# Six of fifteen sums of exps made by accumulating DMAs, in a fused graph network and masked attention kernel

## The chip, the cores and the metric

The kernel runs on one core of a Trainium2 chip. The metric is the device time of one execution in microseconds (us); the time of a kernel is the median of its runs. The engines are TensorE (PE: matmuls; PEld: its weight loads), VectorE (DVE), ScalarE (ACT), GpSimd (POOL) and SyncE (SP, here the issuer of most DMAs). They run side by side, each executing its own instructions in order, and wait for one another through semaphores.

## What is computed

Two layers over x of shape 8 x 2048 x 256 in float32. Layer 0 is a graph convolution with two linear maps and batch norms, layer 1 attention over the graph's edges with 4 heads of 64; each has a residual and a layer norm. The change is in layer 1:

```python
qkv = h @ W                                  # q, k, v: 8 x 4 heads x 2048 x 64
mask = jnp.where(adj == 0, -jnp.inf, 0.0)
scores = jnp.einsum('bhid,bhjd->bhij', q, k) / np.sqrt(HEAD_DIM) + mask
attn = jax.nn.softmax(scores, axis=-1)
out = jnp.einsum('bhij,bhjd->bhid', attn, v)
x = _layernorm(x + out, axis=-1)
```

The softmax needs, for each query, the sum of the exps over all 2048 keys. That sum is what the change moves about.

## The kernel before

The first 1270 us or so are layer 0, which the change doesn't touch. The attention then runs over NU = 64 units (8 batches x 2 pairs of heads x 4 chunks of 512 queries). A unit goes through NT = 16 tiles of 128 keys. Scores are made transposed, keys on the partitions and queries along the free dimension, for two heads at a time, so that a tile of exps, `prob`, is 128 x 2 x 512 float32: 4 KB in each partition, 512 KB in all. The sum over the keys is thus a sum over 16 tiles and then over 128 partitions.

For each step g (tile j of unit u) these functions are issued, in an order written out by hand in the main loop, and every engine keeps it:

- `scores(g + 3)` (L824): four matmuls of 64 x 64 tiles, keys times queries, into PSUM (`st`, two buffers). Scores run LEAD = 3 tiles ahead.
- `mask_scores(g + 3)` (L836): VectorE adds the mask while it takes the scores out of PSUM into a `prob` buffer; there are 13 of these.
- `exps(g + 3)` (L842): ScalarE, in place.
- side tasks, listed by unit and step in `side`: projections of later q, k and v (L765, L779), layer norms, loads, and the end of the unit before.
- `weigh(g)` (L854): TensorE multiplies the exps by v and accumulates in PSUM (`out_ps`). In the last step of a unit it comes before the masks of that step.
- `add_up(g)` (L863, L865): GpSimd adds tile after tile into `acc` (two buffers).

The end of a unit is `finish_sums(u)` at step 4 of the next unit. There TensorE multiplies by a matrix of ones, which sums over the partitions. It does so for every part of the sum that is left: `acc`, and those tiles that GpSimd did not add, whose number is `on_pe(u)`. Each part is four matmuls with 32 columns of ones and 256 columns of data (L881); a float32 matmul shows as two instructions in the records, so a part is 8 of them. ScalarE then copies the sums out (L889), and two steps on they are turned, inverted and applied to the output (L895 to L916). At step 4 after the last unit the same is done for unit 63, with nothing beside it.

So `on_pe` divides the 16 tiles: the first `16 - on_pe(u)` go to GpSimd, the rest to TensorE. Before, it is 4 for the last three units and 1 for all others: a usual unit has 14 adds on GpSimd (tiles 0 to 14) and two parts on TensorE (tile 15 and `acc`).

A `prob` buffer is used again for the tile 13 further on: the mask of tile g + 3, issued in step g, writes into the buffer of tile g - 10, and waits for all that read or write that.

Of the kernel before, what the change touches and what calls it, by code (L numbers as in the profile page):

```python
# [11 lines left out]
ALU = mybir.AluOpType  # L12
# [14 lines left out]
def tile_gcn_then_masked_attention(  # L27
# [15 lines left out]
    nc = tc.nc  # L43
# [7 lines left out]
    NT = N // P  # L51
# [4 lines left out]
    NCH = N // CH  # L56
# [138 lines left out]
    with tc.tile_pool(name="bt7", bufs=1, side="right") as bp7, tc.tile_pool(  # L195
# [20 lines left out]
        for n, t in enumerate(order):  # L216
# [7 lines left out]
            j, m = divmod(t, HT)  # L224
            k, q = divmod(m, TPC)
            here = slice(q * P, (q + 1) * P)
            for g in range(NT // 4):
# [4 lines left out]
                i, m0 = divmod(4 * g, HT)  # L232
# [405 lines left out]
    NU = B * HP * NCH  # L638
# [156 lines left out]
    def attention():  # L795


        with tc.tile_pool(
# [9 lines left out]
            units = [(b, hp, c) for b in range(B) for hp in range(HP) for c in range(NCH)]  # L808
            probs, accs, outs, ots, sts, pms = {}, {}, {}, {}, {}, {}

            def on_pe(u):

                return 4 if u >= NU - NCH + 1 else 1

            def scores(g):
                u, j = divmod(g, NT)
# [40 lines left out]
                        )  # L857

            def add_up(g):
                u, j = divmod(g, NT)  # L860
                if j == 1:
                    accs[u] = ap_.tile([P, 2, CH], F32, name="acc")
                    nc.gpsimd.tensor_add(accs[u], probs[g - 1], probs[g])  # L863
                elif 1 < j < NT - on_pe(u):
                    nc.gpsimd.tensor_add(accs[u], accs[u], probs[g])  # L865

            def finish_out(u):
                ots[u] = ap_.tile([P, CH], F32, name="ot")
                nc.scalar.copy(ots[u], outs[u][:, 0, :])
                nc.vector.tensor_add(ots[u], outs.pop(u)[:, 1, :], ots[u])  # L870

            def finish_sums(u):

                pm = ps_m.tile([P, BR], F32, name="pm")
                parts = [probs.pop(g) for g in range((u + 1) * NT - on_pe(u), (u + 1) * NT)]
                parts.append(accs.pop(u))
                for n, part in enumerate(parts):
                    for h in range(2):
                        for q in range(2):
                            r0 = 32 * (2 * h + q)  # L880
                            nc.tensor.matmul(  # L881
                                pm[r0 : r0 + 32, :], ones[:, :32],
                                part[:, h, q * BR : (q + 1) * BR],
                                start=(n == 0), stop=(n == len(parts) - 1),
                            )
                for g in range(u * NT, (u + 1) * NT - on_pe(u)):
                    del probs[g]
                sts[u] = ap_.tile([P, BR], F32, name="sm")
                nc.scalar.copy(sts[u], pm)  # L889
# [64 lines left out]
            for b in range(B):  # L954
# [3 lines left out]
                for c in range(NCH):  # L958
# [3 lines left out]
                    u = u0 + 3 + c  # L962
# [26 lines left out]
            with tc.manual_schedule(engines=IN_ORDER):  # L989
# [34 lines left out]
                for g in range(NU * NT):  # L1024
                    u, j = divmod(g, NT)
                    ahead = g + LEAD < NU * NT
                    if ahead:
                        st = scores(g + LEAD)
                    if j == NT - 1:
                        weigh(g)  # L1030
                        finish_out(u)
                    if ahead:
                        mask_scores(g + LEAD, st)
                        exps(g + LEAD)
                    for _, f, args in side.get((u, j), ()):
                        f(*args)
                    if j < NT - 1:
                        weigh(g)
                    add_up(g)
# [5 lines left out]
    def attention_with_maxima():  # L1045

        with tc.tile_pool(name="full", bufs=2) as ap_, tc.tile_pool(
# [9 lines left out]
            for b in range(B):  # L1057
# [55 lines left out]
                for c in range(NCH):  # L1113
# [3 lines left out]
                    for half in range(2):  # L1117
                        inp.emit(b, c, half)

    attention()  # L1120


# [62 lines left out]
```

## Time and profile before

| | before |
|---|---|
| median of three runs | 3640.62 us (3638.4 to 3642.35) |
| span of the profiled execution | 3639.4 us |
| TensorE busy | 3587.3 us, 99% |
| GpSimd busy | 2757.1 us, 76% |
| VectorE busy | 1989.5 us, 55% |
| ScalarE busy | 1642.6 us, 45% |
| GpSimd adds into acc (L863, L865) | 887, of 2.36 us each |
| matmul records of L881 on prob / on acc | 584 / 512 |

Busy shares are over the whole span; engines do different things in its parts, so the table of stretches, which gives busy times between two points in time, is the one to argue from. In a line of a group the columns are: source line, engine, operation, output and inputs by the program's names, shapes, number of instructions, and after the bar the busy time in us, the mean of one in ns, and the idle time of the engine just before them with what ended most of it. Timelines give start and length in us; consecutive instructions of one kind are merged. The ends of matmuls are modelled and overlap with what follows, so that differences of starts are the better measure on TensorE.

### The profile page before, as it was taken

What the parts mean: (1) busy time and instruction counts of PE and PEld (TensorE: products, weight loads), DVE (VectorE), ACT (ScalarE), POOL (GpSimd) and SP (SyncE); (2) the same over time, 40 slices, a digit from 0 to 9 for tenths busy, and PEclk for the clock granted to TensorE, in tenths of its full rate; (3) what the DMA queues carried; (4) which work ended last, traced back from release to release, by engine and by line L of the source; (5) the groups of instructions that cost most, each with busy time, mean ns of one, the idle gap of its engine ahead of it and who ended that gap; (6) DMA issues with size and microseconds to landing.
All of it is one profiled execution on the core that took longest, in us unless ns stands there. A gap on an engine that the chain in (4) does not pass through costs nothing.

```text
span 3639.4 us, 55807 instructions
## 1 busy us (share of the span) xinstructions
PE 3587.3 (99%) x23055; PEld 1487.6 (41%) x23055; DVE 1989.5 (55%) x2929; ACT 1642.6 (45%) x2036; POOL 2757.1 (76%) x1457
## 2 busy tenths in 40 slices
PE   8999999999999899999999999999999999999997
PEld 4444444444444443433343433343433334343332
DVE  6212141221146646766766766676676676676665
ACT  5001100110135455655665665565566566556554
POOL 3443263424247678999999999999999999999996
PEclk9999999999999899999999999999999999999998
DMA  9122232230256300000010010010001000000000
GB/s 338 61 75 87 81 133 81 75 98 29 81 204 252 147 1 7 24 30 13 19 42 13 13 36 24 13 36 24 7 30 36 7 24 30 13 19 24 7 1 25
DMA packets 132761, 205.82 MB, mean 57 GB/s; under 512 B 6912, under 2 KB 113936, under 8 KB 122000
## 3 DMA queue, kind: packets, MB, share of 16 engines
q1 hardware_dynamic: 132032, 196.11, 15.6%
q0 software_dynamic: 288, 4.98, 0.4%
q8 instruction: 183, 3.00, 0.3%
q10 hardware_dynamic: 176, 1.06, 0.1%
q14 instruction: 82, 0.67, 0.1%
HBM read 126.62 MB, written 75.51 MB: 56 GB/s over the span
## 4 chain that ended last, share of the span: by engine, by line
PE 96%; POOL 1%; DVE 1%; ACT 1%; DMA 0%; issue 0%; SPq 0%; POOLq 0%; DVEq 0%; ACTq 0%
PE out_ps L854 25%; PE st L824 24%; PE pa L329 21%; PE pm L765 6%; PE ph L362 5%; PE pa L539 5%; PE pm L779 3%; PE pm L881 2%; PE pm L707 1%; PE pm L733 1%; PE ps L231 1%; PE pm L908 1%; PE pm L895 1%; POOL acc L865 1%; PE ph L584 1%; PE pc L241 0%
## 5 line engine op out<-in xcount | busy, mean ns | idle before, releaser
L865 POOL TENSOR_TENSOR acc<-acc,prob 128x1024 f32<-128x1024 f32 x823 | 1947.5, 2366 | 97.8 <-ACT prob L842 40.6
L836 DVE SCALAR_TENSOR_TENSOR prob<-mask,st 128x1024 f32<-128x1024 uint8 x1024 | 1243.3, 1219 | 616.9 <-PE st L824 582.0
L842 ACT ACTIVATE prob<-prob 128x1024 f32<-128x1024 f32 x1024 | 1082.3, 1057 | 945.4 <-DVE prob L836 925.1
L854 PE MATMUL out_ps<-prob,v 64*64 64x512 f32 x8192 | 1077.1, 596 | 1.7 <-DVE ot L870 1.7
L824 PE MATMUL st<-qt,kt 64*64 64x512 f32 x8192 | 1064.2, 590 | 0.1
L329 PE MATMUL pa<-t,x 128*128 128x512 f32 x1792 | 773.2, 594 | 2.7 <-ACT x L305 2.7
L824 PEld LDWEIGHTS st<-qt,kt 64*64 64x64 f32 x8192 | 312.8, 133 | 566.9 <-issue 528.3
L329 PEld LDWEIGHTS pa<-t,x 128*128 128x128 f32 x1792 | 341.3, 191 | 432.6 <-issue 428.4
L854 PEld LDWEIGHTS out_ps<-prob,v 64*64 64x64 f32 x8192 | 284.9, 132 | 511.6 <-issue 412.7
L410 POOL TENSOR_TENSOR ag<-ag,dbc 128x512 f32<-128x512 f32 x16 | 20.2, 1262 | 486.1 <-DVE ag L409 456.6
L366 ACT ACTIVATE h<-ph,b1s 128x512 f32<-128x512 f32 x112 | 77.0, 688 | 404.4 <-PE ph L362 404.4
L765 PE MATMUL pm<-x1t,wq 128*128 128x512 f32 x512 | 247.2, 606 | 0.7 <-ACT x1t L739 0.7
L390 ACT COPY ag<-pa 128x512 f32<-128x512 f32 x16 | 9.4, 586 | 422.7 <-PE pa L329 411.6
L362 PE MATMUL ph<-ag,w1s 128*128 128x512 f32 x448 | 193.4, 592 | 0.0
L863 POOL TENSOR_TENSOR acc<-prob 128x1024 f32<-128x1024 f32 x64 | 151.2, 2362 | 32.5 <-ACT prob L842 31.0
L668 ACT ACTIVATE x<-x,ln_nm,ln_rs 128x256 f32<-128x256 f32 x256 | 137.4, 586 | 9.3 <-POOL ln_nm L664 9.3
L779 PEld LDWEIGHTS pm<-wq,x1t 128*128 128x128 f32 x1024 | 119.3, 192 | 29.3 <-issue 27.3
L367 DVE BATCH_NORM_STATS2 st<-h 128x6 f32<-128x512 f32 x112 | 76.9, 692 | 99.1 <-ACT h L366 99.1
L362 PEld LDWEIGHTS ph<-ag,w1s 128*128 128x128 f32 x448 | 85.1, 190 | 107.1 <-issue 106.9
L779 PE MATMUL pm<-wq,x1t 128*128 128x128 f32 x1024 | 128.4, 278 | 0.3 <-ACT x1t L739 0.3
L765 PEld LDWEIGHTS pm<-x1t,wq 128*128 128x128 f32 x512 | 88.2, 192 | 95.9 <-issue 89.1
L299 POOL TENSOR_TENSOR x<-x,dinv 128x1024 f32<-128x1024 f32 x60 | 116.7, 1966 | 0.0
(137 smaller groups left out, 2425.3 us busy)
## 6 DMA issues: line engine op xcount, KB each, us to landing
x<-in_x_dram SPq DMA_DIRECT2D x92, 512.0 KB, 4.1
h_d<-h SPq DMA_DIRECT2D x28, 1024.0 KB, 3.9
t<-h_d SPq DMA_DIRECT2D x28, 1024.0 KB, 7.9
a<-in_adj_dram SPq DMA_DIRECT2D x16, 1024.0 KB, 5.1
y_d<-ag SPq DMA_DIRECT2D x32, 512.0 KB, 2.7
out_dram<-x SPq DMA_DIRECT2D x32, 512.0 KB, 2.9
yt<-y_d SPq DMA_DIRECT2D x28, 512.0 KB, 3.2
bt_d<-t SPq DMA_DIRECT2D x4, 2048.0 KB, 16.1
```

Of the source, the lines that this page charges most:

```text
L329: nc.tensor.matmul(pa, s.t[:, m, :], t[:, m, :], start=(m == 0), stop=(m == HT - 1))
L362: nc.tensor.matmul(ph, w1s[:, d, f * P : (f + 1) * P], ag[:, d, :], start=(d == 0), stop=(d == ND - 1),)
L539: nc.tensor.matmul(py, w[:, f, :], t[:, f, :], start=(f == 0), stop=(f == 1))
L668: nc.scalar.activation(self.t[:, i, :], self.t[:, i, :], AF.Identity, bias=self.nm[:, i : i + 1], scale=self.rs[:, i : i + 1],)
L765: nc.tensor.matmul(pm, wq[:, d, wcols], xt[:, d, cols], start=(d == 0), stop=(d == ND - 1))
L779: nc.tensor.matmul(pm[:, j * P : (j + 1) * P], xt[:, d, t * P : (t + 1) * P], wq[:, d, wcols], start=(d == 0), stop=(d == ND - 1),)
L824: nc.tensor.matmul(st[r * HD : (r + 1) * HD, h, :], kt[hs, j * P + r * HD : j * P + (r + 1) * HD], qt[hs, cols], start=True, stop=True,)
L836: nc.vector.scalar_tensor_tensor(p, mask[:, j, cols][:, None, :].to_broadcast([P, 2, CH]), MASKED, st, op0=ALU.mult, op1=ALU.add,)
L842: nc.scalar.activation(probs[g], probs[g], AF.Exp)
L854: nc.tensor.matmul(outs[u][hs, r, :], inp.qkv[b, hp][2][rs, j, hs], probs[g][rs, h, :], start=(j == 0), stop=(j == NT - 1),)
L863: nc.gpsimd.tensor_add(accs[u], probs[g - 1], probs[g])
L865: nc.gpsimd.tensor_add(accs[u], accs[u], probs[g])
```

## The change

TensorE gets the `acc` part alone in every unit but the last: `on_pe` becomes 0, and 4 for unit 63. All sixteen tiles are then in GpSimd's sum. To make room on GpSimd, six pairs of tiles, (2, 3), (4, 5) up to (12, 13), are first added to each other by the DMA engines: GpSimd issues a DMA from the second tile's buffer to the first's, SBUF to SBUF, with `accum_op=ALU.add`, and adds the pair's sum to `acc` three steps later. Tiles 0 and 1 start `acc` as before, and tiles 14 and 15 are added one by one. The pair (12, 13) is added in step 0 of the next unit. In unit 63 it is five pairs, up to (10, 11), and tiles 12 to 15 go to TensorE.

The DMA for the pair i, i + 1 overwrites tile i. It stands on GpSimd's queue at step i + 1 and waits for TensorE to have weighed tile i and for ScalarE's exp of tile i + 1. The add of the pair waits for the DMA to have landed.

```diff
+            PAIRS = range(2, NT - 2, 2)
+
             def on_pe(u):
-
-                return 4 if u >= NU - NCH + 1 else 1
+                return 4 if u == NU - 1 else 0
...
             def add_up(g):
+
                 u, j = divmod(g, NT)
+                here = NT - on_pe(u)
                 if j == 1:
                     accs[u] = ap_.tile([P, 2, CH], F32, name="acc")
                     nc.gpsimd.tensor_add(accs[u], probs[g - 1], probs[g])
-                elif 1 < j < NT - on_pe(u):
+                elif j - 1 in PAIRS and j < here:
+                    nc.gpsimd.dma_start(probs[g - 1], probs[g], accum_op=ALU.add)
+                elif PAIRS[-1] + 1 < j < here:
                     nc.gpsimd.tensor_add(accs[u], accs[u], probs[g])
+
+                v, i = divmod(g - 4, NT)
+                if v >= 0 and i in PAIRS and i + 1 < NT - on_pe(v):
+                    nc.gpsimd.tensor_add(accs[v], accs[v], probs[g - 4])
```

## The prediction

> **What bounds the kernel now.** I read the page's busy shares first, then a table of stretches, then the chain of waits, then the timelines of TensorE and GpSimd inside one unit.
>
> Busy shares, on the page:
>
> ```profile
> PE 3587.3 (99%) x23055; PEld 1487.6 (41%) x23055; DVE 1989.5 (55%) x2929; ACT 1642.6 (45%) x2036; POOL 2757.1 (76%) x1457
> ```
>
> The attention stretch alone, from the table of stretches (us, then busy time of PE, PEld, DVE, ACT, POOL, each with its count of instructions):
>
> ```profile
> 1350.00:3560.00 2210.00, 2208.78 (x18777) 871.06 (x18779) 1500.62 (x2213) 1305.31 (x1549) 2093.95 (x1074) 1.00 0.06 20
> ```
>
> TensorE is without gaps there (2208.78 of 2210) and GpSimd comes next (2093.95, 95%). VectorE has 68%, ScalarE 59%, the DMA engines 6%. The chain that ended last is 96% PE and 1% POOL. So time is gained only by taking work from TensorE, and GpSimd has no room for it as it stands.
>
> The costliest groups on GpSimd:
>
> ```profile
> L865 POOL TENSOR_TENSOR acc<-acc,prob 128x1024 f32<-128x1024 f32 x823 | 1947.5, 2366 | 97.8 <-ACT prob L842 40.6
> L863 POOL TENSOR_TENSOR acc<-prob 128x1024 f32<-128x1024 f32 x64 | 151.2, 2362 | 32.5 <-ACT prob L842 31.0
> ```
>
> 14 adds of 2.366 us are 33.1 us of a unit. The TensorE timeline where a unit's sums are taken, first in a usual unit, then in unit 62 (start, length):
>
> ```profile
> 1999.86 1.04 PE L824 MATMUL st<-qt,kt 64*64 64x512 f32 x8
> 2000.83 0.64 PE L881 MATMUL pm<-prob,ones 128*32 128x256 f32 x8
> 2001.29 0.61 PE L881 MATMUL pm<-acc,ones 128*32 128x256 f32 x8
> 2001.83 1.09 PE L854 MATMUL out_ps<-prob,v 64*64 64x512 f32 x8
> ```
> ```profile
> 3594.15 1.93 PE L881 MATMUL pm<-prob,ones 128*32 128x256 f32 x32
> 3595.90 0.61 PE L881 MATMUL pm<-acc,ones 128*32 128x256 f32 x8
> 3596.45 1.09 PE L854 MATMUL out_ps<-prob,v 64*64 64x512 f32 x8
> ```
>
> Starts tell what a part costs: two parts hold TensorE from 2000.83 to 2001.83, 1.00 us; five from 3594.15 to 3596.45, 2.30 us. One part more or less is (2.30 - 1.00) / 3 = 0.433 us. A usual unit, from one such place to the next, takes 35.5 to 37.5 us; the last units, with no projection beside them, about 30.7 with two parts (from 3531.52 to 3562.19).
>
> What the trace shows of DMAs: two issued by GpSimd (its timeline), and landing times (us, last column of the list of issues).
>
> ```profile
> 1240.33 0.96 POOL L628 DMA_DIRECT2D wq<-in_L_gnn_W_dram  x1
> 1241.30 0.58 POOL L629 DMA_DIRECT2D mask<-mask_d  x1
> ```
> ```profile
> y_d<-ag SPq DMA_DIRECT2D x32, 512.0 KB, 2.7
> wq<-in_L_gnn_W_dram POOLq DMA_DIRECT2D x1, 768.0 KB, 4.8
> ```
>
> No DMA before goes SBUF to SBUF, and none adds.
>
> **What the Trainium skill says.** (1) "DMA: Bandwidth & Descriptors", SWDGE vs HWDGE vs iDMA: accumulating is only to be had from GpSimd's queue, where its own cores write the descriptors. The trace agrees that an issue costs GpSimd time: 0.96 and 0.58 us. (2) Same page, Anatomy of one DMA: about 2.0 us fixed plus bytes at 436 GB/s, which gives 3.2 us for 512 KB as a plain copy; the trace has 2.7 us for a copy of that size issued by SyncE, and 4.8 us against a formula's 3.8 for GpSimd's 768 KB. (3) "Collectives: The Full Stack", The bandwidth ceiling: an add in the DMA path costs no cycles of its own but needs two source reads on one ring, so half the rate. Nothing before shows it. (4) "SBUF — State Buffer", Who interferes with whom: DMAs have ports of their own and don't slow engines. Not shown here for such traffic.
>
> **The change part by part.**
>
> *Parts of the sums on TensorE.* Before, units 0 to 60 gave TensorE one tile beside acc, units 61 to 63 four. After, only unit 63 gives four. Removed: 61 x 1 + 2 x 4 = 69 parts of 0.433 us = 29.9 us, all on the path, since TensorE has no gaps. Does a stall take its place? The next out_ps matmuls need exps that were started three tiles earlier (5.2 us at 1.72 us a tile, against a chain of 1.22 us on VectorE and 1.06 on ScalarE), so no.
>
> *GpSimd's adds.* 887 before. After, a full unit has 1 + 6 + 2 = 9 adds, 9 x 2.366 = 21.3 us, and six issues. I take 0.8 us an issue (both ends 0.58 and 0.96 seen for 128 rows or so; up to 1.5 if the second read needs more descriptors), 4.8 us. With the LayerNorm root of 1.8 us that some units have, it is 27.9 us against a unit of 35.1. Busy time is not the limit; order and waits are.
>
> *The new waits.* The DMA for pair i stands at step i+1 and waits for TensorE to have read tile i (it overwrites it) and for the exp of tile i+1. The add of pair i stands three steps later and waits for the landing. GpSimd runs in order, so behind a late landing stand the next DMA issue and the next adds; behind those VectorE (13 prob buffers) and TensorE, which wants acc at step 4 of the next unit.
>
> *Landing time L, from start of issue.* Bytes: 512 KB over 16 engines is 32.8 KB each. The page's main queue moved 196.11 MB in 15.6% of 16 x 3639 us, 21.6 GB/s an engine, so a pass is 1.5 us at most; I take 1.4. Fixed share: 2.7 - 1.4 = 1.3 us for SyncE's copy, to which GpSimd's 0.8 us of descriptors is added, 2.1; or 4.8 - 2.1 = 2.7 from the wq load. One pass gives L = 3.5 to 4.1, two passes (the skill's two reads) 4.9 to 5.5, three passes in series 6.3 to 6.9. I take two passes, L = 5.0.
>
> *GpSimd's sequence over a unit with L = 5.0*, from the issue for pair 2, at the last units' pace of 3.44 us a pair: issues start at 0, 3.44, 7.37, 10.8, 14.7 and 19.0 at the latest; the first add waits until 5.0 and ends at 7.4, the next start at landings 8.4, 12.4, 15.8; then pair 12's issue and five adds in a row (tiles 14, pair 10, 15, pair 12, and the next unit's first), to 30.8, 32.6 with the LayerNorm root. Each us on L adds some 2.25 us to this chain, since two DMAs are in flight and half of the wait shows at each of the pairs.
>
> A usual unit takes TensorE 35.5 - 0.43 = 35.1 us: the chain of 32.6 hides, 2.5 us to spare. The last three or four units take 30.7 - 0.43 = 30.2: there GpSimd falls back by 2.4 us a unit. Some 3.5 units make 8 us that TensorE waits for acc, the last of it just before the final sums (now acc's last add starts at 3611.9 and TensorE's sums at 3614.8, near already).
>
> *VectorE and ScalarE.* Same instructions; a mask's write into a prob buffer waits for a landing instead of a GpSimd add, six steps after the pair's add is due, some 10 us. Cost nothing.
>
> *Sum:* 3640.6 - 29.9 + 8 = 3619 us.
>
> **The rivals.**
>
> *A, slower: the landings become GpSimd's bound.* If the add reads and writes in series, or its rate is lower, L = 6.6 (three passes): the chain is 32.6 + 2.25 x 1.6 = 36.2, 1.1 us over each of 60 usual units = 66, and 6 us over 3.5 last ones = 21; 3640.6 - 29.9 + 87 = 3698. With L = 7.5 it is 3.1 x 60 + 28 - 29.9, about 3825. For it: nothing before shows such a DMA, and the sequence leaves just 1.1 us of L. Against it: the DMA engines are 6% busy there, and the page on reduction says that the add itself is free.
>
> *B, no change.* L near 6.1 (chain 35.1, last units 17 us late), or an issue of 2 us: the 29.9 us are eaten, 3635 to 3645.
>
> *C, all hidden.* One pass, L at most 4: the chain is 30.3, as short as the last units; 3640.6 - 29.9 = 3611.
>
> **How the numbers follow.** The forecast with two passes 0.56, C 0.17, B 0.06, A 0.21. The likeliest is 3619. Low end: C less 2 us of run-to-run spread (3638.4 to 3642.35 before), 3609. High end: into A up to L of about 6.5, 3690; left out are C's lower edge and A beyond it, near 2 in 10. Faster by over 0.2% (below 3633.3) is the forecast and C, 0.73; within, B, 0.06; slower, A, 0.21.
>
> **What would show it right or wrong.** L881 with prob falls from 584 matmul records to some 32, and TensorE's sums take 0.57 us a unit. GpSimd shows 573 adds of 2.37 us, and 383 issues of about 0.8 us that land in about 5 us. Usual units take about 35.1 us. In the last three, adds that wait for landings and a TensorE gap of 2 to 4 us before L881's acc. Wrong: landings above 6 us, GpSimd idle before pair adds in every unit with TensorE waiting for acc; an issue of over 1.5 us; adds or masks that grow longer beside the DMAs.

## The result, and the profile after

| | before | after |
|---|---|---|
| median | 3641.3 us (3638.4 to 3642.35) | 3625.68 us (3622.14 to 3625.93) |
| ratio after / before | | 0.9956, 95% interval 0.9939 to 0.9973 |
| span of the profiled execution | 3639.4 us | 3623.8 us |

The change makes the kernel faster by 15.6 us, 0.44%. A second measurement of the same two kernels gave 3638.62 and 3623.64 us, ratio 0.9954 (0.9940 to 0.9968).

Busy shares of the changed kernel, and its attention stretch in the table of stretches (busy time of PE, PEld, DVE, ACT, POOL):

```profile
PE 3561.4 (98%) x22503; PEld 1470.9 (41%) x22503; DVE 1990.5 (55%) x2929; ACT 1638.1 (45%) x2036; POOL 2357.3 (65%) x1526
```
```profile
1350.00:3560.00 2210.00, 2206.02 (x18498) 863.22 (x18494) 1518.46 (x2243) 1315.29 (x1565) 1728.96 (x1150) 1.00 0.53 108
```

TensorE still has no gaps to speak of in the long middle (2206 of 2210 us), so it still bounds, with less to do. GpSimd fell from 2094 to 1729 us there. The DMA engines went from 6% to 53% busy, and VectorE's and ScalarE's instructions are as long as before (page: a mask 1219 ns, an exp 1057 ns in both kernels). The groups of instructions on GpSimd, and the DMAs with their time to landing:

```profile
L877 POOL TENSOR_TENSOR acc<-acc,prob 128x1024 f32<-128x1024 f32 x383 | 944.9, 2467 | 133.6 <-DMA prob<-prob 123.2
L871 POOL DMA_DIRECT2D prob<-prob x383 | 337.7, 883 | 359.0 <-PE out_ps L858 262.9
L873 POOL TENSOR_TENSOR acc<-acc,prob 128x1024 f32<-128x1024 f32 x126 | 317.2, 2518 | 4.9
```
```profile
prob<-prob POOLq DMA_DIRECT2D x383, 512.0 KB, 4.6
```

An issue holds GpSimd for 0.883 us and lands 4.6 us after it began; that is the median, and single landings in the trace take up to 7.4 us. The adds' means of 2.47 and 2.52 us are no slowing: in the timeline below, an add that follows an issue is recorded as starting before the issue's end (2.66 us from 2003.48, where the issue runs to 2003.75), and those that follow a wait take 2.36 or 2.37. One stretch of GpSimd's timeline in a usual unit:

```profile
2002.88 0.87 POOL L871 DMA_DIRECT2D prob<-prob  x1 [2.17 <-PE out_ps L858]
2003.48 2.66 POOL L877 TENSOR_TENSOR acc<-acc,prob 128x1024 f32<-128x1024 f32 x1
2006.31 0.87 POOL L871 DMA_DIRECT2D prob<-prob  x1 [0.17 <-issue]
2007.94 2.37 POOL L877 TENSOR_TENSOR acc<-acc,prob 128x1024 f32<-128x1024 f32 x1 [0.76 <-DMA prob<-prob]
```

Both waits of the new scheme are to be seen: GpSimd waits for TensorE before it may overwrite a tile, and for landings before it adds. In a usual unit neither reaches TensorE.

**Where the time went.** TensorE's timeline, from the start of one unit's sums to the next, unit beside unit in both kernels:

| stretch | after less before, us |
|---|---|
| up to unit 0's sums | -0.4 |
| 60 units: 60 x -0.43 | -25.8 |
| 8 of these 60 units longer than that | +3.1 |
| units 61 to 63 up to the final sums: parts | -3.9 |
| the same: TensorE stalls, and slower matmuls after one of them | +6.9 |
| final sums, up to the transposes behind them | +2.1 |
| from there to the last instruction | +0.2 |
| last instruction to the end of the span | +2.2 |
| sum | -15.6 |

The saving of 29.7 us (25.8 + 3.9) is there; 14 us of it are given back, most of them at the kernel's end. TensorE there (second number: length; in brackets: idle before, and what ended it):

```profile
3543.84 0.44 PE L907 MATMUL pm<-ident,sm 128*128 128x128 f32 x2 [0.91 <-ACT sm L901]
...
3570.53 0.64 PE L893 MATMUL pm<-acc,ones 128*32 128x256 f32 x8 [0.55 <-POOL acc L877]
...
3578.20 0.44 PE L907 MATMUL pm<-ident,sm 128*128 128x128 f32 x2 [3.44 <-ACT sm L901]
...
3579.01 1.59 PE L858 MATMUL out_ps<-prob,v 64*64 64x512 f32 x8
3580.36 1.95 PE L828 MATMUL st<-qt,kt 64*64 64x512 f32 x8
...
3594.74 1.93 PE L893 MATMUL pm<-prob,ones 128*32 128x256 f32 x32
3596.50 0.61 PE L893 MATMUL pm<-acc,ones 128*32 128x256 f32 x8
3600.72 0.69 PE L907 MATMUL pm<-ident,sm 128*128 128x128 f32 x2 [3.60 <-ACT sm L901]
```

Acc itself is late by half a us. The long waits, 3.44 and 3.60 us, are for ScalarE's copy of the sums (L901); of the 3.60, 1.55 were there before. The waits of 0.91, 0.55 and 3.44 us make 4.9 of the row of 6.9. Some 1.7 us more are no waiting: behind the wait of 3.44 us the matmuls of weighing and scores took 1.59 and 1.95 us where the same take 1.09 and 1.04, and the granted clock was 0.60 from 3579.0 to 3583.3. ScalarE's timeline tells why the copy is late:

```profile
3574.88 1.09 ACT L668 ACTIVATE x<-x,ln_nm,ln_rs 128x256 f32<-128x256 f32 x2 [4.16 <-POOL ln_nm L664]
3575.87 1.04 ACT L846 ACTIVATE prob<-prob 128x1024 f32<-128x1024 f32 x1
3576.82 1.08 ACT L668 ACTIVATE x<-x,ln_nm,ln_rs 128x256 f32<-128x256 f32 x2
3577.80 0.35 ACT L901 COPY sm<-pm 128x256 f32<-128x256 f32 x1
```

ScalarE had stopped 4.16 us for a layer norm's root, which GpSimd makes, and which stood on its queue behind five adds in a row (3560.49 to 3572.80). Exps and the copy of the sums stood behind that on ScalarE.

### The profile page after: what moved, and what is told of

It reads as the page before. It is cut to its first block, busy times and chain, and to the rows that moved or that the text cites. A ratio compares the mean times of both kernels' runs of the same rounds, so it can differ in the third digit from the quotient of the medians.

```text
span 3623.8 us, 55074 instructions
## 1 busy us (share of the span) xinstructions
PE 3561.4 (98%) x22503; PEld 1470.9 (41%) x22503; DVE 1990.5 (55%) x2929; ACT 1638.1 (45%) x2036; POOL 2357.3 (65%) x1526
## 4 chain that ended last, share of the span: by engine, by line
PE 94%; POOL 2%; DMA 1%; DVE 1%; issue 1%; ACT 1%; SPq 0%; POOLq 0%; DVEq 0%; ACTq 0%
PE out_ps L858 24%; PE st L828 23%; PE pa L329 21%; PE pm L765 6%; PE ph L362 5%; PE pa L539 5%; PE pm L779 3%; PE pm L893 1%; DMA prob<-prob 1%; PE pm L733 1%; PE pm L707 1%; POOL acc L877 1%; PE ps L231 1%; PE pm L920 1%; PE pm L907 1%
## 5 line engine op out<-in xcount | busy, mean ns | idle before, releaser
L840 DVE SCALAR_TENSOR_TENSOR prob<-mask,st 128x1024 f32<-128x1024 uint8 x1024 | 1242.9, 1219 | 586.6 <-PE st L828 582.7
L846 ACT ACTIVATE prob<-prob 128x1024 f32<-128x1024 f32 x1024 | 1081.8, 1057 | 922.3 <-DVE prob L840 882.1
L877 POOL TENSOR_TENSOR acc<-acc,prob 128x1024 f32<-128x1024 f32 x383 | 944.9, 2467 | 133.6 <-DMA prob<-prob 123.2
L871 POOL DMA_DIRECT2D prob<-prob x383 | 337.7, 883 | 359.0 <-PE out_ps L858 262.9
L873 POOL TENSOR_TENSOR acc<-acc,prob 128x1024 f32<-128x1024 f32 x126 | 317.2, 2518 | 4.9
```

What stands on the lines that cost most here:

```text
L840: nc.vector.scalar_tensor_tensor(p, mask[:, j, cols][:, None, :].to_broadcast([P, 2, CH]), MASKED, st, op0=ALU.mult, op1=ALU.add,)
L846: nc.scalar.activation(probs[g], probs[g], AF.Exp)
L871: nc.gpsimd.dma_start(probs[g - 1], probs[g], accum_op=ALU.add)
L877: nc.gpsimd.tensor_add(accs[v], accs[v], probs[g - 4])
```

## The experiments

**The last three units as before.** Edit:

```diff
-                return 4 if u == NU - 1 else 0
+                return 4 if u >= NU - NCH + 1 else 0
```

> The change, but with four tiles of each of the last three units on TensorE again (8 parts more, 8 x 0.433 = 3.5 us). Theory: what was lost of the 29.9 us went mostly in the last three units, where GpSimd falls behind a TensorE unit of 30.2 us; with tiles 12 to 15 off its hands it keeps up there, the stalls of some 10 us go, and the time is about 3619 (3616 to 3622). Rival: the loss is spread over all units (DMA traffic slowing the engines); then this only adds its parts, about 3629.

Measured 3622.07 us, ratio to before 0.9947 (0.9933 to 0.9961). Units 62 and 63 are back at the old lengths, with no stall (31.97 and 20.67 us against 31.96 and 20.68). But the time lies just outside the expected range (by 0.07 us), since the end of unit 63, which this edit leaves as it is, keeps its waits:

```profile
3590.76 1.93 PE L893 MATMUL pm<-prob,ones 128*32 128x256 f32 x32
3593.51 0.64 PE L893 MATMUL pm<-acc,ones 128*32 128x256 f32 x8 [0.82 <-POOL acc L877]
3597.91 0.69 PE L907 MATMUL pm<-ident,sm 128*128 128x128 f32 x2 [3.76 <-ACT sm L901]
```

From the start of these sums to the transposes it is 7.2 us; in the change it was 6.0, and before 3.9. So the 6.9 us of units 61 to 63 go when GpSimd has less to add there, and the loss at the final sums stays and grows a little. The medians of this run and of the change, taken on different chips, can't be told apart; the reading rests on the timelines.

**Only the DMAs.** TensorE keeps the parts that it had:

```diff
-                return 4 if u == NU - 1 else 0
+                return 4 if u >= NU - NCH + 1 else 1
```

> The DMAs that add stay, but TensorE keeps as many parts as before the change (one tile in a usual unit, four in the last three). Theory: relieving GpSimd alone gains nothing, since TensorE had no gaps, and the DMAs disturb no engine: the time of before within 0.1%, 3638 to 3645. Rival: the DMA traffic slows masks, exps or matmuls: over 3650. Second rival: part of the gain comes from GpSimd's being free and not from TensorE's parts: under 3634.

Measured 3645.01 us against 3640.18, ratio 1.0013 (1.0007 to 1.0020): at the upper edge of the theory (3645), and slower by a little that is clear of the noise. Usual units are 35.53 and 37.50 us, within 0.01 us of those of before, but for two that are 0.3 and 0.4 us longer: the DMAs disturb no engine there, and relieving GpSimd gains nothing. The little is mostly at the end, where the final sums wait for acc (1.26 us) and then for ScalarE (3.76 us), as in the run with the last three units as before.

**Only the parts, no DMAs.** Edit of the kernel before:

```diff
-                return 4 if u >= NU - NCH + 1 else 1
+                return 4 if u == NU - 1 else 0
```

> The other half alone: all sixteen tiles in GpSimd's sum by 15 plain adds, no DMAs. Theory: 15 x 2.366 = 35.5 us a unit, and 1.8 us more where a layer norm's root is, against TensorE's 35.1 to 37.1: GpSimd becomes the bound in most units by 0 to 2 us, and in the last two by 5 to 7, so the saving of 29.9 is given back: 3635 to 3680. Rival: the buffers even this out and the DMAs were not needed: 3612 to 3626.

Measured 3761.68 us, ratio 1.0335 (1.0320 to 1.0349): the direction of the theory, but 82 us above the upper end of its range. GpSimd's stretch, and TensorE's two large waits in the attention (us in all, times, longest):

```profile
1350.00:3600.00 2250.00, 2152.54 (x17786) 842.55 (x17779) 1460.87 (x2152) 1269.49 (x1517) 2170.85 (x1105) 0.99 0.06 20
```
```profile
PE pm L895 <- ACT sm L889: 71.0, 30, 3.4
PE pm L881 <- POOL acc L865: 47.3, 37, 4.6
```

GpSimd is busier than TensorE now. I had counted the root of 1.8 us for some units. There is a root for each chunk's end and one for each chunk's input, one a unit on average, and some units have two: those take up to 42.2 us. 35.5 + 1.8 = 37.3 us a unit exceeds TensorE's mean of about 36. That makes some 75 us in 60 units, and these take 123 us more than in the change. What the count leaves out is the other wait: TensorE lost more to ScalarE's copy of the sums than to acc, and ScalarE itself waited 113.3 us for the roots, in 32 places. The mean granted clock was also lower, 0.984 against 0.993. How the rest divides between the two is not shown. So the DMAs are what makes this division of the tiles possible.

**Copy instead of add.**

```diff
-                    nc.gpsimd.dma_start(probs[g - 1], probs[g], accum_op=ALU.add)
+                    nc.gpsimd.dma_start(probs[g - 1], probs[g])
...
-                    nc.gpsimd.tensor_add(accs[u], probs[g - 1], probs[g])
+                    nc.gpsimd.tensor_scalar(accs[u], probs[g], 1e-3, None, op0=ALU.add)
```

> The DMAs copy instead of adding (the first tile of each pair is left out of the sum), and acc starts from one tile and a small constant. One look at the landing times. Theory: the accumulate reads twice, so its bytes take two passes, 2 x 1.4 us; a copy takes one and lands 1.3 to 1.5 us sooner, 3.1 to 3.4 us after the issue against 4.6. Rival: the landing is nearly all fixed cost, and the copy takes over 4.2 us.

This is a single execution. Landings and the queue's share of the 16 engines, copying:

```profile
q0 software_dynamic: 55440, 205.81, 14.3%
...
prob<-prob POOLq DMA_DIRECT2D x383, 512.0 KB, 2.9
```

and the queue of the change, adding, with as many packets and bytes:

```profile
q0 software_dynamic: 55440, 205.81, 30.0%
```

A copy lands in 2.9 us, an add in 4.6. The shares, less the 0.4% that this queue had before, give 13.9% x 3616.6 us / 383 = 1.31 us of each engine for a copy, and 29.6% x 3623.8 us / 383 = 2.80 us for an add. That is 2.1 passes. An issue takes 0.582 us on GpSimd for a copy and 0.883 for an add. So adding costs more in both places, on the DMA engines and on GpSimd. What remains of the landing, 1.6 us for a copy and 1.8 for an add, is an estimate of the share that doesn't grow with the bytes; only one size was run. The two source reads that the Trainium skill gives for an add ("Collectives: The Full Stack", The bandwidth ceiling), from which the prediction took its two passes, fit the time of 2.1 passes. That the second pass is a read is not shown: the queue records no more packets or bytes for an add than for a copy.

**The root ahead of the five adds.**

```diff
-                    at_step(u + 2, 2, inp.root, b, c)
+                    at_step(u + 1, 14, inp.root, b, c)
```

> The change, with the layer norm root of a finished unit moved from step 2 of the unit after next to step 14 of the unit before that, ahead of the five adds in a row on GpSimd. Theory: in the last units ScalarE waits for that root (ln_nm) and the copy of the sums stands behind it, which holds TensorE for 3.4 and 3.6 us; with the root early these waits go and acc is no later than before: 4 to 7 us faster than the change, about 3620. Rival: only the lateness of acc counts; then the root just stands in front of the adds, and the time is that of the change or 2 us more, 3625 to 3629.

Measured 3620.59 us, ratio 0.9944 (0.9930 to 0.9957), against the change's 0.9956 and 0.9954: by its size near the theory's (3 to 5 us gained), though the intervals overlap. The timelines are clearer. The one longer unit in each batch is gone (37.07 us, once 37.40, against 37.2 to 38.0), and the last wait for ScalarE fell from 3.60 to 0.49 us. But at the sums of the unit before the last, TensorE now waits for acc:

```profile
3571.81 1.08 PE L893 MATMUL pm<-acc,ones 128*32 128x256 f32 x8 [3.91 <-POOL acc L877]
```

From the sums of unit 60 to those of unit 63 TensorE takes 86.9 us here and 86.3 in the change, so nothing was gained there. The order of GpSimd's work only moves the wait; there is too much of it for a unit of 30.2 us. What was gained is 2.9 us in the 60 units before and 1.5 us at the final sums. Both theories had a part of it.

**A pair's add one step later.**

```diff
-                v, i = divmod(g - 4, NT)
+                v, i = divmod(g - 5, NT)
...
-                    nc.gpsimd.tensor_add(accs[v], accs[v], probs[g - 4])
+                    nc.gpsimd.tensor_add(accs[v], accs[v], probs[g - 5])
```

> The change, with a pair's add five steps after its first tile instead of four, so that it stands behind two more issues and not one. Theory: GpSimd's waits for landings (123 us in all) fall to under 30 us; in usual units TensorE does not feel them, so these keep 35.1 and 37.1 us, and only the last units gain or lose some us (the last add of a unit comes a step later): 3619 to 3629. Rival: the landing waits set the pace in all units: under 3615.

Measured 3687.47 us, ratio 1.0128 (1.0113 to 1.0144): nearly 60 us above the range. GpSimd's waits for landings did go, to nothing that its list of waits shows. In TensorE's waits in the attention stands instead (us in all, times, longest):

```profile
PE pm L907 <- ACT sm L901: 35.5, 31, 3.8
PE pm L893 <- POOL acc L877: 35.3, 42, 2.4
```

In GpSimd's timeline (2005.27 and 2007.59) the last pair is now added after the next unit's first add and not before it, so acc is ready 2.4 us later and more, and usual units grew to 36.1 to 37.3 us where they were 35.1. Half of TensorE's waits are for ScalarE's copy of the sums; ScalarE waited 62.6 us for roots in this run. Acc's due time at step 4 has less room than one add. The waits for landings, 123 us in all, cost next to nothing in usual units, and taking them away in this way cost 62 us.

**A pair's add right behind its issue** (g - 2 in the same two lines).

> The change, with a pair's add one step after its issue, so that no other issue stands between and the whole landing lies open on GpSimd. Theory: each pair then takes 4.6 + 2.4 = 7.0 us in series, six of them 42, with three more adds and a root less one overlapped add some 49 us a unit against TensorE's 35.5: 4350 to 4600 us. Rival: the 13 buffers and the three tiles of lead absorb it: under 3700.

A single execution took 4467.8 us: inside the range. GpSimd waits for landings in 336 places, 1150.7 us in all, in its timeline often 3.8 us before the add of a pair. So in the change most of the 4.6 us of landing is hidden because another issue, and the wait for TensorE before it, stand between.

**Seven pairs.**

```diff
-            PAIRS = range(2, NT - 2, 2)
+            PAIRS = range(2, NT, 2)
```

> The change with seven pairs: tiles 14 and 15 are added by a DMA too, and the pair goes into acc in step 2 of the next unit. Theory: GpSimd has one add of 2.37 us less and one issue of 0.88 us more, and three adds in a row at a unit's end instead of five, so it falls back less in the last units: 2 to 5 us faster than the change, 3620 to 3624; usual units the same. Rival: a later end of acc (step 2) makes TensorE wait at step 4 in every unit: over 3640.

Measured 3623.78 us, ratio 0.9954 (0.9940 to 0.9967). It lies in the theory's range and can't be told from the change. The longer unit in each batch is nearly gone here too, with the root in its old place (one unit is 1.7 us longer, no other by more than 0.3); the last units stall as in the change (86.7 us from unit 60's sums to unit 63's).

**A version put together from these.** Root at step 14, seven pairs, and

```diff
-                return 4 if u == NU - 1 else 0
+                return 6 if u == NU - 1 else 2 if u >= NU - NCH + 1 else 0
```

> Seven pairs, the root at step 14, and two tiles of units 61 and 62 and six of unit 63 on TensorE (6 parts more than the change, 2.6 us). Theory: the stalls of the last units (some 9 us), those of one unit in each batch (3 us) and most of the wait at the end go; 3614 to 3618. Rival: what is lost is not in the order of GpSimd's work but comes with the DMAs; then only the parts are added, 3627.

> The same with six pairs as in the change. Theory: usual units hide GpSimd's five adds in a row, so six or seven pairs make no difference there, and the last units are the same: within 2 us of the run with seven. Rival: the five adds cost something in usual units too: 4 us or more above it.

> The change itself once more, beside the next two on the same chip. Both theories: 3622 to 3627.

On one chip: before 3638.62, the change 3623.64, with seven pairs 3623.23 (ratio to before 0.9952, 0.9938 to 0.9965), with six 3614.06 us (0.9928, 0.9914 to 0.9942). Six pairs beat the change by 9.6 us and before by 24.6. The end of it on TensorE:

```profile
3567.08 1.07 PE L893 MATMUL pm<-prob,ones 128*32 128x256 f32 x16
3567.97 0.61 PE L893 MATMUL pm<-acc,ones 128*32 128x256 f32 x8
...
3586.89 2.80 PE L893 MATMUL pm<-prob,ones 128*32 128x256 f32 x48
3589.51 0.61 PE L893 MATMUL pm<-acc,ones 128*32 128x256 f32 x8
3590.62 0.44 PE L907 MATMUL pm<-ident,sm 128*128 128x128 f32 x2 [0.49 <-ACT sm L901]
```

Of TensorE's waits for acc and for ScalarE's copy 0.49 us is left in the whole attention. It gives TensorE six parts more than the change has, 2.6 us of work, and gets back 12. That the two versions would be within 2 us of one another was wrong. With seven pairs the last add of a unit comes at step 2 of the next, behind that unit's first add, and three units in most batches are 0.3 to 1.5 us longer; TensorE's sums wait for acc 20 times, 8.5 us, and with six pairs not once. It is the same lesson as the later add. Seven pairs with the root in its old place hardly did this (2 us in 60 units, here 10), so the early root has a part in it: it stands ahead of the last adds and waits there for VectorE's statistics, 66.5 us in all. With six pairs it waits as long, 65.3 us, and TensorE feels nothing of it.

## Why the prediction was right, and where not

- **The parts on TensorE:** right. 0.433 us a part was forecast, and the units are shorter by 0.43 us; two parts cost 1.00 us before and one costs 0.57 after. 29.7 of 29.9 us are found in the timeline.
- **Usual units hide GpSimd's chain:** right for all but eight. The runs with only one half of the change show both sides of it: the DMAs alone leave usual units as they were, the parts alone make GpSimd the bound.
- **Landing time:** 5.0 us taken, 4.6 measured as the median; two passes, as chosen, borne out by the copy (2.1). The issue was 0.88 us for 0.8.
- **The last units:** 8 us were forecast, 9.0 measured (6.9 + 2.1). The place is right, and so is the reason that GpSimd has too much to add there: with less of it, the 6.9 us go. The rest is wrong, and that the sizes agree is luck. The prediction said that TensorE waits for acc, in a gap of 2 to 4 us; before the sums of unit 62 it waited 0.55 us for acc, and elsewhere in the last units not at all. For the most part it waited for ScalarE, 6.4 us more than before, which stood still for a layer norm's root behind the adds, and 1.7 us came from the lower clock after such a wait. The root was counted in GpSimd's time, and nobody was named who waits for it. Three and a half units of 30.2 us were counted, too; the trace of before has two (30.67 us, and 31.96 with three parts more), and then a last stretch of 20.68 us. The prediction's own sum with the measured landing time would have been 5 us: (31.7 - 30.2) x 3.5.
- **What was left out:** 3.1 us in one unit or so of each batch, nearly gone when the root stands earlier, and 2.2 us between the last instruction and the end of the span. The forecast gain of 21.6 us became 15.6: these two terms, 5.3 us, and 1 us in the last units make the difference.
- **Rivals:** none came true as told. The median landing stayed under the 6.1 us where usual units were to begin to wait; 30 of the 383 landings took longer, up to 7.4 us, and usual units took no harm that shows beyond the 3.1 us. Rival B's sum is off: 3640.6 - 29.9 + 17 is 3628, not 3635 to 3645. That is near the measured time, but at a landing time that was not there. The run with the add right behind its issue shows what rival A feared: 826 us slower than before once landings lie open (in one execution, at a mean granted clock of 0.913).

The time from TensorE's last instruction to the end of the span was 7.0 us before, 9.2 and 8.9 us in two profiles of the change, 6.9 to 11.1 us in the other kernels with these DMAs, and 6.5 us in the one with the parts alone. The traces show where it goes: GpSimd's closing drain, an instruction on which the last exchange between the engines waits. It takes 3.42 us in both profiles of the change, 1.8 to 5.6 us in the others with these DMAs, and 0.23 us before and with the parts alone. So the term comes with the DMAs. What the drain itself waits for is not shown, nor is how it could be shortened.

## What to carry to other kernels

When work is moved off the engine that bounds, list for the engine that takes it, or issues it, everything else that stands on its queue, and ask for each who waits for it: here the longest waits of the change were for a root of 1.8 us that ScalarE wanted. In the last units, putting the root first only made acc late instead, since the work itself was too much for them. A wait on an engine with time to spare may cost nothing, and taking it away may cost much if it shifts the one result that has a due time. Stages with less to hide behind (the last units) want a setting of their own, and it is cheap to give it to them.

## What the runs showed of the hardware

A DMA issued by GpSimd that adds 512 KB SBUF to SBUF took 4.6 us from issue to landing (median), against 2.9 us for a copy, and 0.88 us of GpSimd against 0.58. It kept each DMA engine busy for 2.80 us, against 1.31 for the copy. With the DMA engines 53% busy in the attention stretch, matmuls, masks, exps and adds kept their durations. Other DMAs in that stretch did not all do so: the store of a finished chunk landed in 5.9 us where it was 2.9 before, the load of x in 6.2 for 3.8; the load of y, 3.3 for 3.2, was hardly slower.

After waits of TensorE of 3.44 and 3.60 us in the change and of 3.91 us with the early root, the granted clock was 0.60, 0.50 and 0.55 over the next few us; after the wait of 1.55 us before, it was 1.00.
